# Routed layers of a decoder: more buffers for gathered rows, selected matrices stored token by token, gates and fetches at other places in the order

## The chip, the cores and the metric

The kernel runs on one core of one Trainium2 chip. The metric is the device time of one execution in microseconds (us), and of several executions the median. The core has five engines that run side by side and wait for each other through semaphores: PE (matrix products, with PEld for the load of its stationary operand), DVE (vector), ACT (scalar, activation functions), POOL (GpSimd) and SP, which here only issues DMAs. Transfers between memory and on-chip buffers are DMAs; those that one engine issues leave its queue in order.

## The reference

A decoder of twelve blocks on x of 32 batches x 128 tokens x 128 features, all in fp32. Each block is `x = x + f(layernorm(x))`. The change touches the sixth, a pair of routed layers (and the place where a small filter for the seventh is computed). Eight rows of 128 features make one routed "token" of 32 x 32 numbers, so there are 512 routed tokens:

```python
def kmoe(x_flat, W_router, A, B, scale, bias, d_in1, d_in2, d_out1, d_out2, top_k):
    logits = x_flat @ W_router.T                  # 64 experts
    vals, idx = jax.lax.top_k(logits, top_k)      # the best 2
    probs = jax.nn.softmax(vals, axis=-1)
    xs = x_flat.reshape(-1, d_in1, d_in2)
    Ag = A[idx]
    Bg = B[idx]
    Y = jnp.einsum('nkoi,nij,nkpj->nkop', Ag, xs, Bg)
    out = jnp.einsum('nkop,nk->nop', Y, probs).reshape(-1, d_out1 * d_out2)
    return out * scale + bias
...
    h = kmoe(x_flat, W_up, A_up, B_up, scale_up, bias_up, D1, D2, F1, F2, TOP_K)      # 32x32 -> 64x64
    h = jax.nn.gelu(h, approximate=False)
    y = kmoe(h, W_down, A_down, B_down, scale_down, bias_down, F1, F2, D1, D2, TOP_K) # 64x64 -> 32x32
```

So every token is multiplied from both sides by the matrices of its two experts, weighted by their shares, first upwards (32 x 32 to 64 x 64) and then downwards.

## The kernel before

The kernel runs the twelve blocks one after the other. Stages up to the fifth run in `stream` (L1493), the routed pair in `l1_ffn` (L2616), the seventh in `l2_attn` (L3059). Here tokens are worked in four blocks k = 0 to 3 of eight batches (128 routed tokens each, one to a partition where tokens lie on partitions), and a block in four quarters m = 0 to 3, each of two batches f.

**Routing upwards** is `routing(k)` (L2554), a generator that does a share of its work at each call. It normalizes eight batches (`xn`), transposes them (`xp`), multiplies by the router (`lp`), takes the best two (`top`), and then, on POOL, gathers the rows of the experts' table by eight indirect DMAs (`whole`, two buffers, L2603), each of which SP stores to a table in memory (`tup`, L2604), one row per token. The shares of the two experts are kept as `R`. For blocks 0 and 1 the shares run inside `stream` (L1798 to L1802), on the steps t at which u is 0, 1, 2, 3, 5, 6 and 7; for blocks 2 and 3 `routed(k)` (L2641) runs the whole of it at one place in `l1_ffn`.

**Upwards product** of a block:

- `fetched(k, m)` (L2645) reads a quarter of the block's table back, with four DMAs of 256 KB issued by SP, into two `gt` tiles. Four such tiles exist.
- `gated(k)` (L2655) spreads the shares `R` over partitions with one matmul (`pr`) and copies them to `gate` on DVE. It also takes the block's buffer for `h`, of which there are two.
- `blocks(k, m)` (L2663) transposes the tokens (DVE) and writes them as block diagonals `bd` (ACT).
- `inner(k, m)` (L2674) multiplies them by one of the matrices (PE, `tp`), and DVE multiplies by `gate` on the way out of PSUM (`tb`). `tp`, `pr`, `xp`, `lp` and the filters' products share two PSUM tiles (`bank`).
- `outer(k, m)` (L2687) multiplies by the other matrix (PE, `hp`, 32x64 pieces); DVE adds the bias into `h`, ACT applies Gelu.

`first(k)` (L2804) runs these for the four quarters; `inner` runs one quarter ahead, and a quarter m + 2 is fetched when `outer(k, m)` is issued.

**Routing downwards**: `logits(k)` (L2706) multiplies `h` by the second router (`lp`), `chosen(k)` (L2719) takes the best two as one-hot rows `oh`, `marked(k)` (L2733) transposes them (`op`, 64x64 matmuls on two diagonal quarters of the array).

**Downwards product**, `second(k)` (L2821):

- `picked(k, n)` (L2753), eight times: a matmul of a slice of all experts' matrices (`tab`, read by `tables`, three buffers) with the one-hot rows gives the chosen experts' matrices of every token (`gp`, a PSUM tile of 128 x 1024). ACT and DVE in turn copy it to `gd[0]` (n < 4) or `gd[1]`.
- `narrowed(k, m, w)` (L2763), eight times: 16 matmuls of 64x64 (`td`; each is two records in the profile), stationary `h` of a token, moving that token's matrix from `gd[0]`. ACT copies the result to `tb` (two copies, tile `td`).
- `spread(k, m, w)` (L2777): 32 matmuls (`yp`; 64 records), stationary that token's matrix from `gd[1]`, moving `tb`.
- `returned(k)` (L2790): DVE transposes `yp` back, adds it to x and takes the statistics of the eight batches for the next layer norm.

In `gd` of before the token is the last axis, so one token's matrix has its elements 64 (and 128) numbers apart:

```python
gd = [one.tile([128, 32, 2, 64], F32, name=f"gd{j}") for j in range(2)]   # [.., column, expert, token]
```

**What sets the order.** `Ordered` (L1355) makes every engine's compute instructions run in the order of the program text; DMAs are placed in SP's queue by a scheduler, mostly as they become ready. So the list at the end of `l1_ffn` (L2836 to L2872) is the order of PE, DVE, ACT and POOL.

**The filters** (`filters`, L3015) compute the seventh block's long filter in three shares, called from `l1_ffn`: loads, then a product `fa` and a sine, then a product `hp1` with a decay and a store to `flt`. They have a pool of their own for `pe`, `tw`, `fw1`, `fw2`, `row`, `arg`, `turn`, `dec` and `w`.

Of the kernel before, what the change touches and what calls it, by code (L numbers as in the profile page):

```python
# [13 lines left out]
F32 = mybir.dt.float32  # L14
# [1352 lines left out]
class Fast(General):  # L1367
# [125 lines left out]
    def stream(self, stages, context=False, fresh=False):  # L1493

        tc, plain = self.tc, self.nc
        nc = self.nc = Ordered(plain, tc)
        M = NB * len(stages)
        with ExitStack() as es:
# [274 lines left out]
            for t in range(-9, M + 11):  # L1773
                n = t - 3
                if 0 <= n < M and n % 2 == 1:
                    outputs(n)
                for fn, at in after:
                    n = t - at
                    if n % 4 == 3 and 0 <= n < M:
                        fn(n // 4)  # L1780
                if context and -3 <= t < NB - 3 and t % 4 == 1:
                    context_group((t + 3) // 4)
                for fn, at in ahead:
                    n = t + at
                    if n % 4 == 0 and 0 <= n < M:
                        if fn is normed and n % NB == 0:
                            T[n // NB] = self.prepared(wk, bank, *stages[n // NB])
                        fn(n // 4)
                if 0 <= t - 1 < M:
                    summed(t - 1)  # L1790
                if 0 <= t < M:
                    scores(t)
                for n in (t - 2, t - 1):
                    if 0 <= n < M and (T[n // NB]["kind"] == "keys") == (n == t - 2):
                        values(n)
                if fresh:
                    for k in range(2):
                        u = t - (M - NB + 8 * k + 13)  # L1798
                        if u == 0:
                            T["route", k] = self.routing(k, bank)  # L1800
                        if u in (0, 1, 2, 3, 5, 6, 7):
                            next(T["route", k], None)  # L1802
        self.nc = plain

# [811 lines left out]
    def l1_ffn(self):  # L2616
# [4 lines left out]
        with ExitStack() as es:  # L2621
# [13 lines left out]
                nc.sync.dma_start(out=t, in_=i[key])  # L2635
                return t

            gd = [one.tile([128, 32, 2, 64], F32, name=f"gd{j}") for j in range(2)]
            A, B, C, D = self.A, {}, {}, {}

            def routed(k):  # L2641
# [3 lines left out]
            def fetched(k, m):  # L2645
                s = A[k]
                for f in range(2):
                    j = 2 * m + f
                    s["gt"][j] = gt = wk.tile([128, 4, 2, 128], F32, tag="gt", name="gt", bufs=4)
                    for c in range(2):  # L2650
                        nc.sync.dma_start(out=gt[:, :, c, :],
                                          in_=s["tab"][c, 16 * j:16 * j + 16].rearrange("(g r) (i c) -> (r i) g c", g=4,
                                                                                        c=128))

            def gated(k):  # L2655
                s = A[k]
                p = bank([128, 64], "pr")
                self.mm(p, self.bg("lup"), s["R"].rearrange("p g k -> p (g k)"))
                s["gate"] = wk.tile([128, 64], F32, tag="gate", name="gate")
                nc.vector.tensor_copy(s["gate"], p)  # L2660
                B[k] = wk.tile([128, 64, 64], F32, tag="h", name="h")

            def blocks(k, m):  # L2663

# [88 lines left out]
            def picked(k, n, eng):  # L2753

                t = T.pop(8 * k + n)
                p = banks([128, 8, 128], "gp")
                for c in range(8):
                    self.mm(p[:, c, :], t[:, c, :], D[k][:, 2 * (n // 4):2 * (n // 4) + 2, :].rearrange("p c t -> p (c t)"))
                eng(gd[n // 4][:, 8 * (n % 4):8 * (n % 4) + 8].rearrange("p c k t -> p c (k t)"), p)
                if 8 * k + n + 3 < 32:  # L2760
                    tables(8 * k + n + 3)

            def narrowed(k, m, w):  # L2763
                h = B[k]
                t0 = 16 * m + 8 * w
                tp = banks([128, 2, 512], "td")
                for u in range(8):
                    for f in range(2):
                        q = slice(64 * f, 64 * f + 64)
                        self.mm(tp[q, f, 64 * u:64 * u + 64], h[q, t0 + u, :],  # L2770
                                gd[0][q, :, :, t0 + u].rearrange("p c k -> p k c"))
                D[k, m, w] = tb = wk.tile([128, 16, 32], F32, tag="td", name="td")
                for f in range(2):
                    q = slice(64 * f, 64 * f + 64)
                    nc.scalar.copy(tb[q], tp[q, f].rearrange("p (u c) -> p u c", c=32))

            def spread(k, m, w):  # L2777
                tb = D.pop((k, m, w))
                if m == w == 0:
                    D["y"] = banks([128, 2, 512], "yp")  # L2780
                yp = D["y"]
                for u in range(8):
                    for c in range(2):
                        for f in range(2):
                            q = slice(64 * f, 64 * f + 64)
                            g, r = 2 * w + u // 4, u % 4
                            self.mm(yp[32 * r:32 * r + 32, f, 128 * m + 32 * g:128 * m + 32 * g + 32],
                                    gd[1][q, :, c, 16 * m + 8 * w + u], tb[q, 2 * u + c, :], start=c == 0, stop=c == 1)

            def returned(k):  # L2790
                yp = D.pop("y")
# [10 lines left out]
                    self.stats(self.X[:, 8 * k + j, :], 8 * k + j)  # L2802

            def first(k):  # L2804
                gated(k)
                inner(k, 0)
                for m in range(4):
                    if m < 3:
                        inner(k, m + 1)
                    if m == 1 and k > 0:  # L2810
                        marked(k - 1)
                    if m < 2:
                        blocks(k, m + 2)
                    outer(k, m)
                    if m < 2:
                        fetched(k, m + 2)
                    if k == 0 and m < 2:
                        next(taps)
                A.pop(k)

            def second(k):  # L2821
# [11 lines left out]
                        marked(3)  # L2833
                returned(k)

            fetched(0, 0)  # L2836
            fetched(0, 1)
            bup, tdn, iota = load("bup", [128, 64]), load("c_tdn2", [128, 64]), load("c_iota", [128, 64])
            wdn = load("wdn", [128, 64, 64])
            taps = self.filters(es, bank)  # L2840
            next(taps)
            for n in range(3):
                tables(n)
            blocks(0, 0)
            blocks(0, 1)
            first(0)
            fetched(1, 0)
            fetched(1, 1)
            routed(2)
            blocks(1, 0)  # L2850
            blocks(1, 1)
            logits(0)
            chosen(0)
            first(1)
            fetched(2, 0)
            fetched(2, 1)
            routed(3)
            blocks(2, 0)
            blocks(2, 1)
            logits(1)  # L2860
            second(0)
            first(2)
            fetched(3, 0)
            fetched(3, 1)
            blocks(3, 0)
            blocks(3, 1)
            logits(2)
            second(1)
            first(3)
            logits(3)  # L2870
# [141 lines left out]
                    normed(g + 2)  # L3012


    def filters(self, es, bank):  # L3015

        nc, tc, i = self.nc, self.tc, self.i
        fp = es.enter_context(tc.tile_pool(name="L2af", bufs=1))
        pe = fp.tile([33, 2, 128], F32, name="pe")
        nc.sync.dma_start(out=pe, in_=i["c_pe"])  # L3020
        tw = fp.tile([128, 2, 128], F32, name="tw")
        nc.sync.dma_start(out=tw, in_=i["c_tw"])
        fw1 = fp.tile([33, 64], F32, name="fw1")
        nc.sync.dma_start(out=fw1, in_=i["fw1"])
        fw2 = fp.tile([64, 256], F32, name="fw2")
        nc.sync.dma_start(out=fw2, in_=i["fw2"])
        row = fp.tile([128, 2, 256], F32, name="row")
        nc.gpsimd.memset(row, 0.0)
        yield
        ap = bank([64, 256], "fa")  # L3030
        self.mm(ap, fw1, pe.rearrange("p n t -> p (n t)"))
        arg = fp.tile([64, 256], F32, name="arg")
        nc.vector.tensor_scalar(arg, ap, self.col("L2a_b1")[0:64], 10.0, ALU.add, ALU.mult)

        turn = fp.tile([64, 256], F32, name="turn")
        nc.vector.tensor_scalar(turn, arg, 1.0 / (2.0 * math.pi), None, ALU.mult)
        nc.vector.tensor_scalar(turn, turn, 12582912.0, None, ALU.add)
        nc.vector.tensor_scalar(turn, turn, 12582912.0, None, ALU.subtract)
# [1 line left out]
            nc.vector.scalar_tensor_tensor(arg, turn, -part, arg, ALU.mult, ALU.add)  # L3040
        nc.vector.tensor_scalar(arg, arg, 3.1415925, -3.1415925, ALU.min, ALU.max)
        nc.scalar.activation(arg, arg, AF.Sin)
        dec = fp.tile([128, 2], F32, name="dec")
        for n in range(2):
            nc.scalar.activation(dec[:, n:n + 1], self.col(f"L2a_fd{n}"), AF.Exp)
        nc.vector.tensor_scalar(dec, dec, -1.0, None, ALU.mult)
# [1 line left out]
        for n in range(2):  # L3048
            hp = bank([128, 128], "hp1")
            self.mm(hp, fw2[:, 128 * n:128 * n + 128], arg[:, 128 * n:128 * n + 128])  # L3050
            w = fp.tile([128, 128], F32, name=f"w{n}")
            nc.scalar.activation(w, tw[:, n, :], AF.Exp, scale=dec[:, n:n + 1])
            nc.vector.scalar_tensor_tensor(w, hp, self.col(f"L2a_b2{n}"), w, ALU.add, ALU.mult)
            nc.vector.tensor_scalar(row[:, n, 127 * n:127 * n + 128], w, self.col(f"L2a_fb{n}"), 1.0 / 128.0,
# [182 lines left out]
```

## Time and profile before

| what | value |
|---|---|
| runs | 5709.6, 5717.45, 5721.61 us; median 5717.45 us |
| profiled execution | 5707.47 us, its span 5705.6 us |
| PE busy over the span | 5085.8 us (89%) |
| routed layers in the span | 807 to 1232 us |
| first(0), first(1), first(2), first(3): first `tp` to end of last `hp` | 816.3 to 857, 877.9 to 925.7, 1001.6 to 1038.9, 1094.0 to 1134 us |
| logits(0) to (3) start | 867.3, 935.6, 1041.3, 1135.5 us |
| second(0), second(1): first `gp` to end of last `yp` | 945.1 to 1001.4, 1050.8 to 1093.7 us |
| second(2), second(3) | 1145.0 to 1187.9, 1187.9 to 1230.4 us |

The profile is of one execution; times in it count from the span's start. A row of its timeline gives start and length in us, the engine, the line of the program, the operation with the names of what it writes and reads, its shape and a count, and in brackets how long the engine was idle before it and what ended that. L1350 is a helper through which most instructions pass, and L363 is another, so rows are told apart by their tiles. PE's rows of a group overlap, so the distance from the start of one group to the start of the next says more than the length of one record.

### The profile page before, as it was taken

What the parts mean: (1) busy time and instruction counts of PE and PEld (TensorE: products, weight loads), DVE (VectorE), ACT (ScalarE), POOL (GpSimd) and SP (SyncE); (2) the same over time, 40 slices, a digit from 0 to 9 for tenths busy, and PEclk for the clock granted to TensorE, in tenths of its full rate; (3) what the DMA queues carried; (4) which work ended last, traced back from release to release, by engine and by line L of the source; (5) the groups of instructions that cost most, each with busy time, mean ns of one, the idle gap of its engine ahead of it and who ended that gap; (6) DMA issues with size and microseconds to landing.
All of it is one profiled execution on the core that took longest, in us unless ns stands there. A gap on an engine that the chain in (4) does not pass through costs nothing.

```text
span 5705.6 us, 143617 instructions
## 1 busy us (share of the span) xinstructions
PE 5085.8 (89%) x56814; PEld 3543.7 (62%) x56814; DVE 4246.9 (74%) x11606; ACT 2931.8 (51%) x4110; POOL 3053.6 (54%) x4772
## 2 busy tenths in 40 slices
PE   8976976777877999886899999999999999999998
PEld 4533556664555666664666666666666666676665
DVE  5577642345529999986888888888888888888885
ACT  5756752233525555543455555555555555555554
POOL 0042011011014555555777778778778777777774
PEclk9988987798989999998999999999999999999999
DMA  1000055233002222211334444444444444444442
GB/s 50 2 1 1 2 182 190 83 94 111 9 11 57 51 50 52 51 46 47 65 63 83 83 76 70 76 82 72 72 84 74 72 82 75 72 71 71 74 72 54
DMA packets 1807432, 376.01 MB, mean 66 GB/s; under 512 B 1681459, under 2 KB 1786394, under 8 KB 1805727
## 3 DMA queue, kind: packets, MB, share of 16 engines
q1 hardware_dynamic: 1797376, 330.90, 28.6%
q10 hardware_dynamic: 4766, 19.06, 1.0%
q0 software_dynamic: 4608, 16.78, 0.9%
q8 instruction: 451, 7.39, 0.6%
q14 instruction: 231, 1.88, 0.1%
HBM read 124.02 MB, written 41.16 MB: 29 GB/s over the span
## 4 chain that ended last, share of the span: by engine, by line
PE 37%; DVE 11%; SPq 7%; POOL 5%; DMA 4%; issue 3%; ACT 2%; DVEq 0%; ACTq 0%; POOLq 0%
SPq L2039 7%; PE sc L1350 6%; PE y L1350 6%; PE qk L1350 5%; PE av L1350 5%; PE vp L1350 4%; DMA qkT<-bt 3%; POOL rt L1350 2%; POOL raw L1350 2%; DVE bt L1350 2%; PE gp L1350 2%; PE oTp L1350 2%; PE ap L1350 1%; DVE neg L1350 1%; DVE ss L1350 1%
## 5 line engine op out<-in xcount | busy, mean ns | idle before, releaser
L1350 POOL TENSOR_TENSOR raw<-raw,rt 128x1024 f32<-128x1024 f32 x384 | 899.0, 2362 | 0.0
L1350 POOL TENSOR_TENSOR raw<-raw,ry 128x2048 f32<-128x2048 f32 x224 | 811.3, 3622 | 14.0
L1350 PE MATMUL qk<-wqkv,zs 128*128 128x512 f32 x1536 | 724.3, 594 | 7.5 <-DVE raw L1350 7.5
L1350 ACT ACTIVATE sq<-qk 128x1024 f32<-128x1024 f32 x448 | 458.6, 1024 | 362.9 <-PE qk L1350 152.5
L1350 POOL TENSOR_TENSOR rt<-ry 128x32 f32<-128x32 f32 (+1 forms) x864 | 198.7, 230 | 797.2 <-DVE ry L1350 688.6
L1350 DVE TENSOR_REDUCE ss<-sq 128x16 f32<-128x1024 f32 x448 | 532.9, 1194 | 46.7 <-ACT sq L1350 46.7
L1350 DVE TENSOR_TENSOR rt<-qk,tab 128x1024 f32<-128x1024 f32 x384 | 468.6, 1220 | 61.3 <-ACT sq L1350 43.3
L1350 DVE STREAM_TRANSPOSE bt<-raw 128x1024 f32<-128x1024 f32 x384 | 455.0, 1221 | 69.2 <-POOL raw L1350 45.0
L1350 DVE TENSOR_TENSOR raw<-qk,tab 128x1024 f32<-128x1024 f32 x384 | 466.9, 1216 | 0.0
L1350 ACT ACTIVATE PT<-sc 128x1024 f32<-128x1024 f32 x384 | 373.0, 1027 | 139.4 <-PE sc L1350 139.1
L1350 PEld LDWEIGHTS qk<-wqkv,zs 128*128 128x128 f32 x1536 | 273.9, 191 | 263.4 <-issue 254.7
L1350 ACT ACTIVATE P<-sc 128x1024 f32<-128x1024 f32 x384 | 373.2, 1021 | 117.4 <-PE sc L1350 116.8
L1350 ACT COPY oT<-oTp 128x512 f32<-128x512 f32 x384 | 208.3, 588 | 438.1 <-PE oTp L1350 437.9
L1350 PE MATMUL sc<-qkT 64*128 64x128 f32 x6144 | 406.8, 283 | 7.5 <-DMA qkT<-bt 1.5
L1350 PEld LDWEIGHTS sc<-qkT 64*128 64x128 f32 x6144 | 374.1, 193 | 59.0 <-issue 53.3
L1350 PE MATMUL vp<-wqkv,zs 128*128 128x512 f32 x768 | 404.5, 608 | 1.4 <-DVE raw L1350 1.4
L1350 PE MATMUL av<-va,P 128*64 128x65 f32 x12288 | 401.1, 223 | 0.0
L1350 PE MATMUL y<-wo,oT 128*128 128x128 f32 x3072 | 392.4, 281 | 0.0
L1350 PEld LDWEIGHTS y<-wo,oT 128*128 128x128 f32 x3072 | 364.7, 193 | 42.2 <-issue 24.8
L1350 PEld LDWEIGHTS av<-va,P 128*64 128x64 f32 x12288 | 374.5, 137 | 23.2 <-issue 0.2
L1350 ACT COPY va<-vp 128x1024 f32<-128x1024 f32 (+1 forms) x232 | 218.0, 940 | 214.3 <-PE vp L1350 214.1
L1350 POOL TENSOR_TENSOR X<-X,brep 128x512 f32<-128x512 f32 x24 | 30.5, 1271 | 512.4 <-DVE xn L1350 512.4
(414 smaller groups left out, 10768.5 us busy)
## 6 DMA issues: line engine op xcount, KB each, us to landing
qkT<-bt SPq DMA_DIRECT2D x3072, 64.0 KB
rows<-scr SPq DMA_DIRECT2D x32, 672.0 KB
tup<-whole SPq DMA_DIRECT2D x32, 512.0 KB
gt<-tup SPq DMA_DIRECT2D x64, 256.0 KB
tab<-in_tdo SPq DMA_DIRECT2D x32, 512.0 KB
T<-flt SPq DMA_DIRECT2D x16, 1024.0 KB
wqkv<-in_dqkv ACTq DMA_DIRECT2D x6, 1536.0 KB
scr<-dots SPq DMA_DIRECT2D x128, 66.0 KB
```

The source lines that it names most:

```text
L1350: self.last = call(*a, **k)
L2039: nc.sync.dma_start(out=qkT[r:r + 32, :, j, :], in_=bt[32 * j:32 * j + 32, o])
```

## The change

- `gt` has six buffers in place of four. `fetched(k, 0)` to `fetched(k, 2)` are called ahead of `first(k)`, and `fetched(k, 3)` inside it after `outer(k, 0)`. For blocks 2 and 3 the three calls stand between `logits(k - 1)` and `second(k - 2)`.
- `gd` has the token as its first axis, then expert, then column. The copies out of PSUM still read it from end to end, so that two neighbours in PSUM (one column of two tokens) are written 64 numbers apart; `narrowed` and `spread` read one token's matrix as contiguous numbers.
- `gated(k)` is called ahead of the block: for block 0 before the fetches, for 1 before `logits(0)`, for 2 and 3 after `logits(1)` and after `first(2)`. The buffer for `h` is now taken in `first(k)`.
- `routed(3)` moves from before `blocks(2, 0)` to between `second(0)` and `first(2)`.
- `filters` keeps its tiles as pieces of one `h` buffer (`room`) in place of a pool; its loads follow the first three fetches in the text, where `bup`, `tdn` and `iota` stand between them.
- In `stream` the shares of `routing` run at u = 0 to 6 with no step left out.

```diff
-                        if u in (0, 1, 2, 3, 5, 6, 7):
+                        if 0 <= u < 7:
                             next(T["route", k], None)
...
-            gd = [one.tile([128, 32, 2, 64], F32, name=f"gd{j}") for j in range(2)]
+            gd = [one.tile([128, 64, 2, 32], F32, name=f"gd{j}") for j in range(2)]
...
-                    s["gt"][j] = gt = wk.tile([128, 4, 2, 128], F32, tag="gt", name="gt", bufs=4)
+                    s["gt"][j] = gt = wk.tile([128, 4, 2, 128], F32, tag="gt", name="gt", bufs=6)
...
                 nc.vector.tensor_copy(s["gate"], p)
-                B[k] = wk.tile([128, 64, 64], F32, tag="h", name="h")
...
-                eng(gd[n // 4][:, 8 * (n % 4):8 * (n % 4) + 8].rearrange("p c k t -> p c (k t)"), p)
+                eng(gd[n // 4][:, :, :, 8 * (n % 4):8 * (n % 4) + 8].rearrange("p t k c -> p c k t"), p.rearrange("p c (k t) -> p c k t", k=2))
...
                         self.mm(tp[q, f, 64 * u:64 * u + 64], h[q, t0 + u, :],
-                                gd[0][q, :, :, t0 + u].rearrange("p c k -> p k c"))
+                                gd[0][q, t0 + u])
...
-                                    gd[1][q, :, c, 16 * m + 8 * w + u], tb[q, 2 * u + c, :], start=c == 0, stop=c == 1)
+                                    gd[1][q, 16 * m + 8 * w + u, c, :], tb[q, 2 * u + c, :], start=c == 0, stop=c == 1)
...
             def first(k):
-                gated(k)
+                B[k] = wk.tile([128, 64, 64], F32, tag="h", name="h")
...
                     outer(k, m)
-                    if m < 2:
-                        fetched(k, m + 2)
+                    if m == 0:
+                        fetched(k, 3)
...
+            gated(0)
             fetched(0, 0)
+            bup, tdn, iota = load("bup", [128, 64]), load("c_tdn2", [128, 64]), load("c_iota", [128, 64])
             fetched(0, 1)
-            bup, tdn, iota = load("bup", [128, 64]), load("c_tdn2", [128, 64]), load("c_iota", [128, 64])
+            fetched(0, 2)
+            taps = self.filters(wk.tile([128, 64, 64], F32, tag="h", name="room"), bank)
+            next(taps)
             wdn = load("wdn", [128, 64, 64])
-            taps = self.filters(es, bank)
-            next(taps)
...
             first(0)
-            fetched(1, 0)
-            fetched(1, 1)
+            for m in range(3):
+                fetched(1, m)
             routed(2)
             blocks(1, 0)
             blocks(1, 1)
+            gated(1)
             logits(0)
             chosen(0)
             first(1)
-            fetched(2, 0)
-            fetched(2, 1)
-            routed(3)
             blocks(2, 0)
             blocks(2, 1)
             logits(1)
+            gated(2)
+            for m in range(3):
+                fetched(2, m)
             second(0)
+            routed(3)
             first(2)
-            fetched(3, 0)
-            fetched(3, 1)
+            gated(3)
             blocks(3, 0)
             blocks(3, 1)
             logits(2)
+            for m in range(3):
+                fetched(3, m)
             second(1)
...
-    def filters(self, es, bank):
+    def filters(self, room, bank):
...
+        room = room.rearrange("p t c -> p (t c)")
+        at = [0]
+
+        def piece(n, *shape):
+            size = math.prod(shape)
+            at[0] += size
+            t = room[0:n, at[0] - size:at[0]]
+            return t if len(shape) == 1 else t.rearrange("p (a b) -> p a b", a=shape[0])
+
-        pe = fp.tile([33, 2, 128], F32, name="pe")
+        pe = piece(33, 2, 128)
```

The other tiles of `filters` become pieces in the same way.

More of the change, by code (lines that the diff above doesn't have):

```diff
@@ L3012, in l2_ffn @@
                     normed(g + 2)
-    def filters(self, es, bank):
+    def filters(self, room, bank):
         nc, tc, i = self.nc, self.tc, self.i
-        fp = es.enter_context(tc.tile_pool(name="L2af", bufs=1))
-        pe = fp.tile([33, 2, 128], F32, name="pe")
+        room = room.rearrange("p t c -> p (t c)")
[6 more added lines that the diff above has]
+        pe = piece(33, 2, 128)
         nc.sync.dma_start(out=pe, in_=i["c_pe"])
-        tw = fp.tile([128, 2, 128], F32, name="tw")
+        tw = piece(128, 2, 128)
         nc.sync.dma_start(out=tw, in_=i["c_tw"])
-        fw1 = fp.tile([33, 64], F32, name="fw1")
+        fw1 = piece(33, 64)
         nc.sync.dma_start(out=fw1, in_=i["fw1"])
-        fw2 = fp.tile([64, 256], F32, name="fw2")
+        fw2 = piece(64, 256)
         nc.sync.dma_start(out=fw2, in_=i["fw2"])
-        row = fp.tile([128, 2, 256], F32, name="row")
+        row = piece(128, 2, 256)
         nc.gpsimd.memset(row, 0.0)
@@ L3031, in filters @@
         self.mm(ap, fw1, pe.rearrange("p n t -> p (n t)"))
-        arg = fp.tile([64, 256], F32, name="arg")
+        arg = piece(64, 256)
         nc.vector.tensor_scalar(arg, ap, self.col("L2a_b1")[0:64], 10.0, ALU.add, ALU.mult)
-        turn = fp.tile([64, 256], F32, name="turn")
+        turn = piece(64, 256)
         nc.vector.tensor_scalar(turn, arg, 1.0 / (2.0 * math.pi), None, ALU.mult)
@@ L3042, in filters @@
         nc.scalar.activation(arg, arg, AF.Sin)
-        dec = fp.tile([128, 2], F32, name="dec")
+        dec = piece(128, 2)
         for n in range(2):
@@ L3050, in filters @@
             self.mm(hp, fw2[:, 128 * n:128 * n + 128], arg[:, 128 * n:128 * n + 128])
-            w = fp.tile([128, 128], F32, name=f"w{n}")
+            w = piece(128, 128)
             nc.scalar.activation(w, tw[:, n, :], AF.Exp, scale=dec[:, n:n + 1])
```

## The prediction

> **What bounds the kernel now.** The page's slices place the routed layers (L1 FFN) at 807 to 1232 us of the span; PE is their engine, at a lower clock than around them. The waits of PE in 805:1235 say what it lacks (waiter, releaser, us in total, times, longest):
>
> ```profile
> PE tp L1350 <- DMA gt<-tup: 54.0, 10, 14.4
> PE gp L1350 <- DMA tab<-in_tdo: 15.1, 11, 7.5
> PE tp L1350 <- DVE gate L1350: 11.6, 3, 5.1
> ```
>
> Gathered rows that have not landed cost PE 54.0 us. The stage windows then set second(0) beside second(1), the same work (length, then busy us and count of PE, PEld, DVE, ACT and POOL, granted clock, DMA share, GB/s):
>
> ```profile
> 945.10:1001.40 56.30, 44.83 (x903) 42.16 (x901) 7.33 (x18) 15.53 (x21) 7.98 (x7) 0.88 0.57 198
> 1050.80:1093.70 42.90, 40.85 (x903) 38.49 (x900) 7.33 (x18) 16.66 (x22) 0.00 (x0) 1.00 0.33 101
> ```
>
> Where routed(3) gathers beside it, second(0) takes 13.4 us more; where nothing does, PE is busy 40.85 of 42.90 us. There the matmuls themselves count. The timeline of PE in second(2) (start, us, count at the end):
>
> ```profile
> 1175.07 1.35 PE L1350 MATMUL yp<-td,gd 64*32 64x32 f32 x64
> 1176.34 0.68 PE L1350 MATMUL op<-ident,oh 64*64 64x64 f32 x16
> 1176.86 1.92 PE L1350 MATMUL td<-gd,h 64*64 64x64 f32 x32
> 1178.71 1.33 PE L1350 MATMUL yp<-td,gd 64*32 64x32 f32 x64
> ```
>
> op and td are the same 64x64 f32 product on the same two diagonal quarters of the array. From the start of op's loads (1176.34) to those of td (1176.80) is 0.46 us, 28.8 ns for each of 16; td runs from there to 1178.71, 59.7 ns each of 32. td differs in one thing: its moving operand is read from gd with 256 and 512 bytes between elements.
>
> **Selected matrices token by token.** A block k has 256 td records (8 x 32). If contiguous reading gives them op's rate, that is 256 x (59.7 - 28.8) = 7.9 us; the bound on the other side is 0. yp reads gd as its stationary operand, 512 records a block at 1.26 us per 64 (1208.54 to 1209.80), 19.7 ns. The nearest contiguous small product is hp (32x64), 128 in 1.46 us, 11.4 ns; so yp saves 0 to 8.3 ns, and I take 3.7 ns, 1.9 us, nearer to no gain because the other strided stationary operand (yp of L3144, 32 loads in 1.04 us) is hardly slower than the contiguous u of L2979 (28 in 0.80, 28.6 against 32.5 ns). Two gaps come back: td no longer covers ACT's two copies of td (1.19 us and 0.17 to start), 0.4 us ahead of the first yp and 0.6 ahead of the last, 1.0 us.
>
> The price is the 8 gd copies, which now write every element 256 bytes from the last:
>
> ```profile
> L3156 DVE TENSOR_TENSOR X<-yt,X 128x512 f32<-128x512 f32 x16 | 19.3, 1217 | 28.0 <-PE yt L3153 28.0
> L1350 DVE COPY gd<-gp 128x1024 f32<-128x1024 f32 x16 | 19.5, 1222 | 36.5 <-PE gp L1350 36.5
> L1350 ACT COPY gd<-gp 128x1024 f32<-128x1024 f32 x16 | 16.2, 1012 | 73.2 <-PE gp L1350 73.2
> ```
>
> L3156 writes (and reads) with 512 bytes between elements: 2.38 ns an element against 1.19 for the copy. Bounds: no change, or double, 2.4 us on DVE and 2.0 on ACT; I take double. PE makes a gp in 1.8 us and each engine copies every other one, so 2.4 of 3.6 us is covered by three PSUM tiles; only the copy behind chosen (n = 5) ends late, 17.65 us into the block where td wants its tile at 17.4: 0.35 us a block. Net 7.9 + 1.9 - 1.0 - 0.35 = 8.4 us a block, **33.6 us** in four.
>
> The Trainium skill ("TensorE: Matmul & The Clock Gate", "Wait — 56ns, not 53.3ns?") speaks against the yp part: starts of matmuls never come closer than about 25 ns however short they are. The hp row, 11.4 ns, denies that here; by the rule yp would save nothing and the sum would end 7.6 us higher. Another page ("SBUF — State Buffer", Door 1) has 16-byte lines with a penalty for every access that leaves one, which would slow ACT's copies too; no row here has ACT writing so, and the page gives no size.
>
> **Fetched rows, gate, order.** Times run forward through the stage. In the changed program's SP queue fetches of gt stand thus: (0,0) to (0,2) at once; (0,3), (1,0) to (1,2) all before the stores of routed(2); (1,3) behind five and six of these; (2,0) to (2,2) behind all; then the tabs of second(0); then two stores of routed(3), three DMAs of (2,3), two stores, the fourth of (2,3), and the rest.
>
> First(0): the four filter loads went ahead of gt on SP (809.99 to 812.21); now gt goes first, 2.2 us. The rest of first(0) hangs on the filters' chain DVE-ACT-DVE (arg, Sin, dec, w with table loads between), which I leave, plus 0.5: **2.7 us**. Nothing hides these loads' new place, but fa wants them only at 830; and the h buffer they lie in is read last by the flt store, issued at 848, while block 1 writes it from 886.
>
> First(1): gate's 1.4 us and the 14.4 us wait for (1,2) go. Next late is (1,3), whose DMAs take the queue places that (1,2)'s had (issued 894.79 and 897.17; tp at 901.75 and 905.30 to 907.3). With the start 2.7 earlier inner(1,3) ends at 904.6, and hp of 2 and 3 take 6.4 us (919.3 to 925.7): 911.0 against 925.7, 14.7, of which 2.7 is counted: **12.0 us**.
>
> Routed(3) leaves its place: logits(1) began 9.9 us after first(1) ended (925.7 to 935.59); without it, it waits 2.4 us for the last Gelu (as 1038.9 to 1041.27) and 0.4 for the gate's matmul: **7.1 us**. Second(0) loses its neighbour: 13.4, less 1.0 for the gt loads that now land beside it: **12.4 us**.
>
> Routed(3) at its new place, counted from the end of second(0)'s last yp: returned(0) holds DVE 6.1 us (1001.47 to 1007.6), the root 2.4, then xp, as at 928.44 to 935.6, 7.2: lp ends at 16.1. First(2) runs m = 0 to 2 by 27. But the fourth DMA of (2,3) stands behind the fourth store of gathered rows; gathers start at 17.5 and the fourth store left 18.6 us after the first gather (937.40, 956.06). It is issued at 36.1, lands 4.6 later (897.17 to 901.75), then tp 2.0 and hp 4.9: 47.6, against 37.6 (1001.35 to 1038.9). **Loss 10.0 us**; the gate ahead gains nothing here. The stores behind clear by 57, ahead of second(1)'s first new tab at 59.
>
> First(3): gate is ready, but tb still queues on DVE behind returned(1), to 6.2 us; hp(0) ends at 12.3 (13.4 before), (3,2) is there, (3,3) is issued at 12.4 and lands by 16.2 (1107.23 to 1111.05 then). Ends at 23, lp at 25.6 against 41.75 (1093.73 to 1135.48): **16.0 us**.
>
> Earlier shares of routing(0) and (1) cost and bring nothing: their gathers already waited for rows (8.8 and 9.1 us idle on POOL) and then for their two buffers. X<-X,brep slides behind four gathers, some 17 us on POOL; its reader X<-X,y comes some 17 steps of 3.6 us later.
>
> **Sum.** 33.6 + 2.7 + 12.0 + 7.1 + 12.4 - 10.0 + 16.0 = 73.8 us. The profiled execution took 5707.47 (span 5705.6 and 1.9 around it), so 5633.7; it lies 10.0 below the median of 5717.45. Against the median: **5644 us**. Later stages keep their order and move earlier as a whole.
>
> **Rivals.** *The stride is not what slows td.* For it: td waits for nothing else, but its array tiles alternate otherwise than op's within u. Then the layout gives nothing and costs 1.4: 73.8 - 33.6 - 1.4 = 38.8 gained, 5679. *The gathers hold the fetches.* For it: SP is one queue and (1,3), (2,3) stand behind gathers whose pairs take some 10 us. If both wait one pair longer and second(0) keeps half its loss, 10 + 10 + 6.2 fall away: 47.6 gained, 5670. *Slower: copies to strided addresses become the bound.* Place: picked, DVE with four copies and some 3 us of chosen in 17.4 us. It shows above (17.4 - 3)/4 = 3.6 us a copy, and undoes 73.8 us when a block gets 18.5 us longer, at (17.4 + 18.5 - 3)/4 = 8.2 us, 8 ns an element; at 8.5 us the time is 5722 or more, at 10 us 5746. The only strided row has 2.38. *The queue does not do what it says* is the second rival.
>
> **Numbers.** Forecast 0.64 (own range 5612 to 5664: yp at hp's rate gives 17 - 7.6 = 9 us more, and a gather chain without neighbours some 10 to 20), stride 0.14, gathers 0.12, slower copies 0.06, no change 0.04 (both first rivals, 12.6 us left, with copies near 4 us). Faster by over 0.2% (about 11 us, what a measurement of this kernel can tell from no change) 0.90, within 0.04, slower 0.06. The range takes in the first two rivals: 5612 to 5686.
>
> **What would show it.** Right: td near 29 ns a record and yp below 20; gd copies near 2.4 (DVE) and 2.0 us (ACT); second blocks of 34 to 35 us at clock 1.0; PE's wait for gt down from 54 to some 25 us, most in first(1) and first(2); none for gate. Wrong: td still near 60 ns; gd copies above 3.6 us; PE waiting in picked; first(2) longer than 50 us after second(0).

## The result and the profile after

The changed kernel takes 5675.1 us (median of 5666.02, 5673.17, 5677.04 and 5678.12), beside 5719.19 us for the kernel before: a ratio of 0.9924, 95% interval 0.9908 to 0.994. It is faster by some 44 us; the forecast was 73.8. The profiled execution took 5678.12 us, its span is 5676.3.

Two profiled executions differ outside the routed layers too, by up to 17 us (below), so I compare the stage itself: from PE's first `pr` row to the end of its last `yp`. It lasted 423.2 us before (807.2 to 1230.4) and 373.1 after (811.6 to 1184.7): 50.1 us less. The kernel after, profiled a second time, had 372.7. The places at which the parts below begin and end are rounded to 0.1 us. The last `hp` of first(0), first(1) and first(3) before ends at 856.1, 924.4 and 1133.2 us (the table ahead of the prediction has 857, 925.7 and 1134).

| part of the stage, us | before | after | gained | forecast |
|---|---|---|---|---|
| start to end of first(0) | 48.9 | 41.3 | 7.6 | 2.7 |
| to end of first(1) | 68.3 | 56.7 | 11.6 | 12.0 |
| to second(0) | 20.7 | 12.1 | 8.6 | 7.1 |
| second(0) | 56.3 | 39.7 | 16.6 | 12.4 + 8.4 |
| first(2) | 37.5 | 51.1 | -13.6 | -10.0 |
| logits(2) | 11.9 | 11.8 | 0.1 | 0 |
| second(1) | 43.0 | 43.1 | -0.1 | 8.4 |
| first(3), logits(3) | 51.2 | 39.3 | 11.9 | 16.0 |
| second(2) | 42.9 | 39.2 | 3.7 | 8.4 |
| second(3) | 42.5 | 38.8 | 3.7 | 8.4 |
| sum | 423.2 | 373.1 | 50.1 | 73.8 |

Outside the second blocks 26.2 us came, where 27.8 were forecast. In the four second blocks 23.9 came, where 46.0 were forecast. The waits of PE in the routed layers after (waiter, releaser, us in total, times, longest):

```profile
PE tp L1350 <- DMA gt<-tup: 19.7, 6, 8.7
PE yp L1350 <- issue: 15.7, 13, 2.2
PE xp L1350 <- DVE xn L1350: 12.9, 2, 8.9
...
PE gp L1350 <- DMA tab<-in_tdo: 7.9, 10, 3.0
```

The wait for gathered rows fell from 54.0 to 19.7 us and that for gate is gone, both as forecast. New is the second line: `yp` waits 15.7 us for *issue*, that is, for nothing that the profile shows. The timeline of PE in second(3) after (start, us, then the count and the idle time ahead of the row) says where:

```profile
1166.29 1.15 PE L1350 MATMUL td<-gd,h 64*64 64x64 f32 x32
1167.37 0.75 PE L1350 MATMUL yp<-td,gd 64*32 64x32 f32 x58
1169.40 0.31 PE L1350 MATMUL yp<-td,gd 64*32 64x32 f32 x6 [1.28 <-issue]
1169.64 1.15 PE L1350 MATMUL td<-gd,h 64*64 64x64 f32 x32
1170.72 0.81 PE L1350 MATMUL yp<-td,gd 64*32 64x32 f32 x64
1171.46 1.02 PE L1350 MATMUL td<-gd,h 64*64 64x64 f32 x26
1172.88 0.44 PE L1350 MATMUL td<-gd,h 64*64 64x64 f32 x6 [0.39 <-issue]
1173.25 0.82 PE L1350 MATMUL yp<-td,gd 64*32 64x32 f32 x64
1173.99 1.15 PE L1350 MATMUL td<-gd,h 64*64 64x64 f32 x32
1175.07 0.37 PE L1350 MATMUL yp<-td,gd 64*32 64x32 f32 x26
1176.62 0.54 PE L1350 MATMUL yp<-td,gd 64*32 64x32 f32 x38 [1.19 <-issue]
```

Both products became faster: 32 td in 1.08 us (1166.29 to 1167.37), 33.8 ns each where it was 59.7; 64 yp in 0.74 us (1173.25 to 1173.99), 11.6 ns where it was 19.7. But PE stops in the middle of a group, and in these rows always after the same number of records: 6 + 32 + 64 + 26 = 128 from 1169.40 to the next stop, 6 + 64 + 32 + 26 = 128 from 1172.88 to the one after. So td and yp of a block take 21.6 us (1163.08 to 1184.7) where they took 25.5, though the array needs only 256 x 33.8 + 512 x 11.6 ns = 14.6 us.

The copies to gd are longer, as forecast (from the groups with their shapes kept apart):

```profile
L1350 ACT COPY gd<-gp 128x1024 f32<-128x1024 f32 x16 | 30.8, 1926 | 58.7 <-PE gp L1350 58.7
...
L1350 DVE COPY gd<-gp 128x1024 f32<-128x1024 f32 x16 | 30.3, 1916 | 26.8 <-PE gp L1350 26.7
```

ACT 1012 to 1926 ns, DVE 1222 to 1916. Both still wait for PE ahead of a copy, so they cost next to nothing: the eight gp of second(3) take 17.2 us (1145.92 to 1163.08), and took 17.0.

### The profile page after: what moved, and what is told of

Its sections match the earlier page's. It is cut to its first block, busy times and chain, and to the rows that moved or that the text cites. A ratio compares the mean times of both kernels' runs of the same rounds, so it can differ in the third digit from the quotient of the medians.

```text
span 5676.3 us, 143617 instructions
## 1 busy us (share of the span) xinstructions
PE 5058.5 (89%) x56814; PEld 3507.2 (62%) x56814; DVE 4265.4 (75%) x11606; ACT 2940.2 (52%) x4110; POOL 3060.3 (54%) x4772
## 3 DMA queue, kind: packets, MB, share of 16 engines
q8 instruction: 451, 7.39, 0.6%
## 4 chain that ended last, share of the span: by engine, by line
PE 35%; DVE 11%; SPq 9%; POOL 5%; DMA 4%; issue 4%; ACT 2%; DVEq 0%; ACTq 0%; POOLq 0%
SPq L2039 8%; PE sc L1350 6%; PE y L1350 5%; PE qk L1350 5%; PE av L1350 4%; PE vp L1350 4%; DMA qkT<-bt 3%; POOL rt L1350 2%; DVE bt L1350 2%; POOL raw L1350 2%; PE gp L1350 2%; PE oTp L1350 2%; PE ap L1350 1%; DVE ss L1350 1%; PE tp L1350 1%
## 5 line engine op out<-in xcount | busy, mean ns | idle before, releaser
L1350 DVE STREAM_TRANSPOSE bt<-raw 128x1024 f32<-128x1024 f32 x384 | 455.6, 1222 | 75.5 <-POOL raw L1350 44.3
```

What stands on the lines that cost most here:

```text
L1350: self.last = call(*a, **k)
```

## The experiments

The theory formed from these rows is **supply**: with the stride gone, PE runs dry of instructions. The page lists the transfers that carry them:

```profile
span 5676.3 us, 143617 instructions
...
q8 instruction: 451, 7.39, 0.6%
```

The trace's records of this queue are packets of 16384 bytes, and in the last 21.5 us of the stage five of them are all that q8 moves. PE has 56814 matmul and 56814 load instructions; 7.39 MB over these are 65 bytes each, so a packet holds 256 instructions, that is 128 records with their loads: the distance between the stops. A packet came every 3.4 to 3.8 us there, some 14 ns an instruction, or 21.5 us for the 1536 of a block's td and yp. The rival is the prediction's own theory, in which the **array** sets the time of these records.

### The layout alone

```diff
 # the kernel before, with
-gd = [one.tile([128, 32, 2, 64], F32, name=f"gd{j}") for j in range(2)]
+gd = [one.tile([128, 64, 2, 32], F32, name=f"gd{j}") for j in range(2)]
 # and its one write (picked) and two reads (narrowed, spread) as in the kernel after
```

> The kernel before with one part of the change alone: the selected matrices gd stored token by token (four lines). The prediction's theory (the time of a block's td and yp records is the array's, set by the stride of their operands) puts this part at 8.4 us a block, 33.6 us in all: 5685 us beside 5719, a ratio of 0.994. The theory formed after the result (with the stride gone, the supply of instructions to PE is the bound: about 14 ns for each of the 1536 instructions of a block's td and yp, 21.5 us where the part took 25.5) puts it at about 4 us a block, 12 to 17 us in all: 5702 to 5707 us, 0.997 to 0.998. The rival that the stride is not what slows td puts it at nothing or at 1 to 3 us a block lost to the slower copies: 5719 to 5731 us.

Measured: 5701.95 us beside 5719.76, a ratio of 0.9967 (0.9956 to 0.9978), 17.8 us; the stage 407.4 us, 15.8 less than before. That is just above what supply gives and half of what the prediction did. In the four blocks the td and yp part took 20.9 to 22.1 us, where it had taken 25.6 to 26.1: 17.2 us less in all.

### All but the layout

```diff
 # the kernel after, with
-gd = [one.tile([128, 64, 2, 32], F32, name=f"gd{j}") for j in range(2)]
+gd = [one.tile([128, 32, 2, 64], F32, name=f"gd{j}") for j in range(2)]
 # and its write and reads as in the kernel before
```

> The kernel after with the old layout of gd: six buffers, gate rows ahead, filters in the free buffer and the new order alone. If the parts add, the prediction's theory (layout worth 33.6 us) gives 5675 + 34 = 5709 us, 0.998 of the kernel before; the theory of instruction supply (layout worth 12 to 17 us) gives 5687 to 5692 us, 0.995, and then the fetching and the order carry most of the gain. The rival that the layout is worth nothing gives 5675 us.

Measured: 5690.63 us, 0.9949 (0.9935 to 0.9963), 29.1 us less than before; the stage 387.4 us. With the new layout 14.3 us of stage follow. The parts add: 15.8 + 35.8 = 51.6 in the stage, 50.1 together.

### Every yp twice

```diff
-                for u in range(8):
+                for u in [u for u in range(8) for _ in range(2)]:
                     for c in range(2):          # in spread
```

> The kernel after with each token's yp matmuls issued twice over (the second pair overwrites the first with the same sums): 512 more matmuls, 1024 more instructions a block, and no other change. Theory of the array's time: 512 x 11.6 ns = 5.9 us a block, 24 us in all: 5699 us. Theory of instruction supply, 14 ns an instruction: 1024 x 14 = 14.3 us a block, 57 us in all: 5732 us; the waits of PE on nothing but issue in td and yp grow by 8 us a block, and the part takes 36 us where it took 21.6.

Measured: 5727.1 us, 1.0014 (1.0005 to 1.0024), 52.0 us over the kernel after, and 5 short of what supply says. The td and yp part took 34.7 to 36.5 us a block, and PE's waits for issue in td and yp rose from 18.3 to 46.2 us. Its timeline in second(3), where nothing else is fetched:

```profile
1207.66 0.44 PE L1350 MATMUL td<-gd,h 64*64 64x64 f32 x6 [1.07 <-issue]
1208.03 1.51 PE L1350 MATMUL yp<-td,gd 64*32 64x32 f32 x122
1211.13 0.31 PE L1350 MATMUL yp<-td,gd 64*32 64x32 f32 x6 [1.59 <-issue]
1211.37 1.15 PE L1350 MATMUL td<-gd,h 64*64 64x64 f32 x32
1212.45 1.75 PE L1350 MATMUL yp<-td,gd 64*32 64x32 f32 x90
1214.60 0.91 PE L1350 MATMUL yp<-td,gd 64*32 64x32 f32 x38 [0.41 <-issue]
```

From stop to stop 128 records each (6 + 122; 6 + 32 + 90) and 3.47 us each, 27.1 ns a record, whether the records are mostly yp or part td. (Of the eight distances between stops in this block seven are 3.47 us and one is 3.75; in the kernel after they were 3.5 to 4.0.) The page of this kernel:

```profile
span 5713.7 us, 147713 instructions
...
q8 instruction: 467, 7.65, 0.6%
```

4096 more instructions, 16 more packets: 256 in each. And the DMA view of 1201.6 to 1236.3 us has one burst of 19 GB/s in every fourth slice of 0.87 us (9 is a small packet of another queue):

```profile
GB/s 0 0 0 19 0 0 0 0 19 0 0 0 19 0 0 0 19 0 0 0 19 0 0 0 19 0 0 0 19 0 0 0 19 0 9 0 19 0 0 0
```

By the records, a packet lands in some 1 us and PE goes on 1.3 to 1.4 us after that (landed 1206.3, 1209.7 and 1213.2; PE at 1207.66, 1211.13 and 1214.60); the next leaves 1.1 to 1.2 us later. So of the 3.5 us the bytes take about 1; the rest passes between a packet's landing and the next one's start. Supply is shown: the array's theory gave 24 us more, supply 57, and 52.0 came. (A kernel with fewer instructions in this part was not run.)

### td among gp

```diff
-                D[k, m, w] = tb = wk.tile([128, 16, 32], F32, tag="td", name="td")
+                D[k, m, w] = tb = wk.tile([128, 16, 32], F32, tag="td", name="td", bufs=3)
...
-                narrowed(k, 0, 0)
+                    if n > 4:
+                        narrowed(k, (n - 5) // 2, (n - 5) % 2)
                 for m in range(4):
                     for w in range(2):
-                        if (m, w) != (3, 1):
-                            narrowed(k, m + w, 1 - w)
                         spread(k, m, w)
+                        a = 2 * m + w + 3
+                        if a < 8:
+                            narrowed(k, a // 2, a % 2)
```

> The kernel after with the td products of the first three steps put behind gp number 5, 6 and 7 (three td buffers in place of two): the same instructions, but 192 of the dense ones stand among the sparse gp ones. Theory of instruction supply: 192 x 14 ns = 2.7 us a block at most, 5 to 11 us in all: 5664 to 5670 us; waits of PE on nothing but issue shrink. Theory of the array's time: no gain (the same records on the same array), 5673 to 5678 us. Rival: PSUM tiles of gp and td hold each other, 0 to 8 us slower.

Measured: 5668.28 us beside 5713.09, 0.9922 (0.9908 to 0.9935), the ratio of the kernel after; the stage 372.6 us. My expectation was wrong. It counted three groups of td, but the third stands behind the last gp, where it stood; two are among gp now. PE in second(3):

```profile
1161.57 1.15 PE L1350 MATMUL td<-gd,h 64*64 64x64 f32 x32
1162.65 2.05 PE L1350 MATMUL gp<-om,tab 128*128 128x128 f32 x16
1164.63 1.15 PE L1350 MATMUL td<-gd,h 64*64 64x64 f32 x32
1165.71 2.05 PE L1350 MATMUL gp<-om,tab 128*128 128x128 f32 x16
1167.69 1.15 PE L1350 MATMUL td<-gd,h 64*64 64x64 f32 x32
```

The part behind the last gp fell from 21.6 to 18.9 us (1167.8 to 1186.7): 2.7, of which 64 records at 27.1 ns are 1.7. But the gp part grew from 17.2 to 19.9. PE is already busy there, so the two td cost their array time of 1.08 us each, which the stops had hidden. The rest of the 2.7 stands elsewhere: the first three gp took 1.3 us longer, at a granted clock of 0.80 (1147.9 to 1155.0; 1.00 after), and the waits for `tab` were 0.9 shorter. All four second blocks took 159.9 us, after 160.7. td is bound by the array (33.8 ns against 27.1 of supply), yp by supply (11.6 against 27.1): only yp would gain among gp, and it can't go there, because it needs its block's last gp. (One block's yp among the next block's gp was not tried.)

### Six buffers undone

```diff
-                    s["gt"][j] = gt = wk.tile([128, 4, 2, 128], F32, tag="gt", name="gt", bufs=6)
+                    s["gt"][j] = gt = wk.tile([128, 4, 2, 128], F32, tag="gt", name="gt", bufs=4)
```

> The kernel after with four buffers of gathered rows in place of six, all else as in after. Theory (the third quarter's early fetch is what the fetching part of the change lives on): the waits of up to 14.4 us for it in first(1), and its like in first(2) and first(3), come back: 15 to 30 us slower than after, 0.995 to 0.9975 of before. Rival (the last quarter, which stands behind the stores of the routing in SP's queue, is the bound anyway): 0 to 5 us slower, 0.9925 to 0.9935.

Measured: 5708.23 us beside 5715.89, 0.9986 (0.9977 to 0.9995), and 40.6 us over the kernel after on the same chip (5667.67); the stage 407.3 us, 34.2 longer. The waits of PE:

```profile
PE tp L1350 <- DMA gt<-tup: 65.8, 14, 12.0
```

More than before had (54.0), and more is lost than the 15 to 30 us expected. So everything that is not layout needs the six buffers to gain anything: with four, the new order, gate and filters leave the stage at 407.3 us, what the layout alone gives (407.4). Six buffers in the order of before were not run, so how much they bring without the new order is open.

### Gate back

```diff
             def first(k):
+                if k > 0:
+                    gated(k)
...
-            gated(1)
-            gated(2)
-            gated(3)
```

> The kernel after with the gate rows of blocks 1 to 3 taken at the start of first(k) again, not a block ahead. PE's waits for gate were 11.6 us in the kernel before (three, up to 5.1). The prediction's steps put 1.4 us of that to the gate's account in first(1) and nothing in first(2) and first(3), where tb queues on DVE behind the same returned(k) anyway: 1 to 3 us slower than after, 0.9925 to 0.993 of before. Rival (the whole wait comes back): 10 to 12 us slower, 0.994 to 0.9945.

Measured: 5667.58 us, 0.9918 (0.9904 to 0.9931), the time of the kernel after on that chip; the stage 371.7 us. PE waits 5.9 us for gate again (three times, up to 3.9), and loses nothing by it: the 4.9 us that `tp` waits for `tb` in the kernel after are not among the waits of this one. As the prediction had it, or less.

### Last quarters from ACT's queue

```diff
                     for c in range(2):
-                        nc.sync.dma_start(out=gt[:, :, c, :],
+                        (nc.scalar if m == 3 else nc.sync).dma_start(out=gt[:, :, c, :],
```

> The kernel after, with the last quarter's gathered rows (fetched(k, 3)) issued from ACT's DMA queue in place of SP's. Theory of the queue: in first(1) and first(2) these transfers stand on SP behind stores of the routing that are not ready, and PE waits 8.7 + 1.6 us and 3.3 + 5.0 us for them; issued from ACT, which is past its work for the quarter then, the waits go: 10 to 18 us less, 5657 to 5665 us. Rival (the transfers are late because the DMA engines are busy with the gathers, wherever they are issued): the waits stay, 5671 to 5679 us. Second rival: ACT's queue holds its own later work (bd, the copies of td) until the buffers come free: up to 5 us slower.

Measured: 5672.0 us, 0.9911 (0.9895 to 0.9926); the stage 372.0 us, 1.1 less than after. The mechanism is there and the gain isn't. In first(2) the waits for (2,3) fell from 3.3 + 5.0 us to 0.5, and second(1) began 203.1 us into the stage, not 212.7. Its PE:

```profile
1018.63 5.62 PE L1350 MATMUL gp<-om,tab 128*128 128x128 f32 x48
1037.03 6.13 PE L1350 MATMUL gp<-om,tab 128*128 128x128 f32 x32 [12.77 <-DMA tab<-in_tdo]
```

and SP's queue at that time:

```profile
1023.04 1.59 SPq L2604 DMA_DIRECT2D tup<-whole  x2
1024.72 5.98 SPq L2651 DMA_DIRECT2D gt<-tup  x8
1030.80 18.54 SPq L2750 DMA_DIRECT2D tab<-in_tdo  x8
```

The next `tab` stands in SP's queue behind routed(3)'s last stores and eight fetches, so it left at 1030.80 whenever PE came for it. Second(1) lasted 51.6 us (43.1 after), which gives 8.5 of the 9.6 us back. Earlier in the stage the same happens: first(1) became 5.5 us shorter and first(0) 5.0 longer, where ACT stood idle for 3.1 us while it issued the block's last fetches (836.05 to 841.17) and PE waited 4.1 us for ACT's `room` (1.7 after), as the second rival has it.

### routed(3) in shares

```diff
 # in second(k), behind spread(k, m, w)
+                        next(route, None)     # route = self.routing(3, bank) for k == 0
...
             second(0)
-            routed(3)
```

> The kernel after with routed(3) not run whole behind second(0) but in seven shares, one after each of the first seven spreads of second(0). Theory (routed(3) in one piece behind second(0) makes PE wait: 8.9 us for xn behind returned(0), 3.3 + 5.0 us for gt(2,3) behind its stores, 3.0 us for tab in second(1)): most of these 20 us go, less what seven shares add to PE and DVE inside second(0), 2 to 4 us: 5655 to 5663 us beside 5675. Rival (gathers beside second(0) slow PE as they did in the kernel before, 13 us): the gain is eaten, 5670 to 5680 us.

Measured: 5659.69 us beside 5713.09, 0.9907 (0.9891 to 0.9922); the stage 364.6 us, 8.5 less than after. (The intervals of the ratios of this kernel and the one after overlap; the gain shows in the stage, which two profiles of the kernel after have at 373.1 and 372.7.) Second(0) lasts 43.8 us (39.7 after), first(2) 43.4 (51.1), second(1) 38.5 (43.1). The wait of 8.9 us for `xn` is gone, and that for `tab` nearly; the waits for (2,3) are not:

```profile
991.27 2.05 PE L1350 MATMUL tp<-gt,bd 128*128 128x128 f32 x8 [5.50 <-DMA gt<-tup]
1000.34 2.05 PE L1350 MATMUL tp<-gt,bd 128*128 128x128 f32 x8 [7.02 <-DMA gt<-tup]
```

### The edits together

```diff
+                        (nc.scalar if m == 3 else nc.sync).dma_start(out=gt[:, :, c, :],
...
+                        next(route, None)     # routed(3) in shares; its own call goes
...
+                            narrowed(k, (n - 5) // 2, (n - 5) % 2)     # td among gp: in the first kernel alone
```

> The kernel after with three edits together: the last quarter's fetches from ACT's queue, routed(3) in shares inside second(0), and three td products among gp. Alone, the first moved its 10 us of waits for gt to a wait for tab in second(1) of 12.8 us, behind the stores of routed(3). If the shares bring these stores forward, both gains stay: 8 (queue) + 15 (shares) + 5 to 10 (mixing) = 28 to 33 us, 5642 to 5650 us. Rival (the gathers of routing(3) beside second(0) take back what the shares bring): 5660 to 5668 us.

> The kernel after with two of the three edits, without the td products among gp: last quarters from ACT's queue and routed(3) in shares inside second(0). Mixing alone moved nothing in a block (38.8 us with and without). If that holds here too: as with all three, a ratio of 0.988 to 0.990 to the kernel before, 5650 to 5658 us. If mixing did bring its 5 to 10 us: 0.990 to 0.992.

Measured: with all three 5650.77 us beside 5713.09, 0.9887 (0.9872 to 0.9902), stage 359.8 us; with two 5658.06 beside 5715.89, 0.9892 (0.9877 to 0.9907), stage 363.9 us. The queue brings next to nothing beyond the shares (364.6 to 363.9). With mixing the stage is 4.1 us shorter here and was 0.5 shorter alone, but not where mixing acts: the four second blocks took 170.4 us with it and 163.4 without, while first(1) and first(2) took 77.1 and 88.9. No run shows why those two became shorter, and the intervals of the ratios overlap, so what mixing brings is open. All three together make the fastest kernel of this study; their interval lies below that of the kernel after on the first chip and overlaps that of its second measurement.

### The kernel after again

> The kernel after once more, beside the three others on their chip. If the differences of 5 to 15 us between the profiles outside the routed layers (start at 807 to 815 us, rest of 4475 to 4492 us) are from execution to execution, this profile shows other values than the first, with a stage of 372 to 374 us again, and the ratio stays at 0.991 to 0.994. If the 4 us later start belongs to the changed kernel, it is there again.

Measured: 5667.67 us beside 5715.89, 0.9909 (0.9894 to 0.9924). The stage took 372.7 us, the rest behind it 4485.3. Over all profiles the stage began between 807.2 and 815.5 us (before's own order 807.2 and, with the layout alone, 811.8; after's 811.6 and 815.0, and 808.2 with four buffers), and what follows took 4475 to 4492 us, with the same code. So the 4.4 us that the first profile after began later are not shown to be a cost of the change, and before's profiled execution was one of its quick ones.

## Why the prediction was right in sign and wrong in size

- **Layout, 33.6 us: the step that failed.** Measured 14.3 to 17.8 us. The array did its part: td saves 256 x (59.7 - 33.8) = 6.6 us a block (7.9 forecast; inside a group its records do start at op's rate, two every 58 ns, and the change from group to group adds the rest) and yp 512 x (19.7 - 11.6) = 4.1 (1.9 forecast; the range to 8.3 held it). The copies stayed below what I took, and hidden, and PE waited 1.4 us in all four blocks for the copies of td, not 1.0 in each. But the step subtracted the saving from the block as if nothing lay below. Of 10.7 us saved on the array 3.9 arrive (25.5 to 21.6), since 768 records at 27.1 ns are 20.8 us whatever the array does. The bursts that I read the rates from (16 op, 128 hp) are at most one packet long, so they could not show a rate that binds over hundreds of records. The page of before showed the packets of q8 (451), and the step had no term for them.
- **Second(1), 8.4 us forecast, 0.1 lost.** The layout gave 3.4 of it (46.5 us without it), and 3.5 were lost: routed(3)'s stores and the fetches of block 3 ran beside it, and a `tab` behind them came 3.0 us late. The step had the stores clear ahead of the first new tab, and counted nothing for the fetches.
- **First(2), -10.0 forecast, -13.6 measured.** The chain was the right one (returned(0) on DVE, xn, gathers, stores, the last fetch of (2,3)); PE waited 8.9 us for xn and 8.3 for (2,3).
- **First(1) 12.0, routed(3) leaving its place 7.1, second(0) without its neighbour 12.4:** measured 11.6, 8.6 and, in the kernel without the layout, 13.3 (43.0 us for 56.3). Right. The 7.1 took first(1) to end at 925.7, where DVE's last row for `h` ends; its last `hp` ends at 924.4, and the same step from there gives 8.3.
- **Start 2.7:** 7.6 came. The step counted the order of the first loads and no wait for rows. PE's waits for `gt` in first(0) fell from 14.1 to 1.1 us, and a wait of 6.8 for `bd` stands in place of the first; with four buffers first(0) took 46.5 us and waited 12.4 for `gt`. **First(3) 16.0:** 11.9; PE still waits 4.9 us for tb there. The two errors nearly cancel.
- **Gate:** nothing, as the steps had it from first(2) on; in first(1) not even its 1.4.
- **The rivals.** "The stride is not what slows td" gave 5679, near the result, by a wrong mechanism: the stride did slow td, and a second limit took over. The measured 5675.1 us lies outside the range of the forecast itself (5612 to 5664) and inside the whole range only because that takes in the first two rivals, neither of which is what happened: so far it is luck. "The gathers hold the fetches" gave 5670, and has a part: the 3.6 us of first(2) and the wait in second(1), not the 26 it charged. "Copies become the bound" is refuted at 1.92 us a copy. The second blocks took 38.8 to 43.1 us, not 34 to 35, and their clock is not why:

```profile
921.70:961.40 39.70, 33.27 (x902) 30.67 (x901) 10.20 (x20) 18.46 (x22) 0.00 (x0) 0.91 0.35 108
...
1145.90:1184.70 38.80, 31.38 (x908) 28.99 (x896) 13.29 (x30) 17.02 (x20) 0.00 (x0) 1.00 0.23 71
```

At a granted clock of 1.00 second(3) is 0.9 us faster than second(0) at 0.91, and PE is busy for 31.38 of its 38.80 us. Of the 7.4 us idle there, 5.0 are five stops for issue (1.28, 0.39, 1.19, 1.18, 0.93).

## What to carry to other kernels

A saving per record ends where the next limit begins: for many small matmuls in a row, count the instructions and set them against the rate at which their packets come (here 256 in 3.47 us), before adding up what the array saves. A wait marked as issue that returns after a fixed number of records points to that limit. And a transfer moved out of a queue in which it stood behind others shows what stands there next, so follow the queue up to the next block before booking the gain.

## What the runs showed of the hardware

- PE's instructions arrive in packets of 16384 bytes, 256 instructions. Where PE uses them up faster, it runs at 3.47 us a packet in the kernel with every yp twice, 13.6 ns an instruction or 27.1 ns a record with its load, of which the transfer itself is some 1 us.
- The Trainium skill ("TensorE: Matmul & The Clock Gate", "Wait — 56ns, not 53.3ns?") has starts of matmuls no closer than about 25 ns. Records of yp come 11.6 ns apart in bursts, closer than that, and 27.1 ns apart over a long run, by supply. But neighbouring records of yp and hp go to different pieces of the array (`f` and `r` in `spread` and `outer`), so their mean does not test the figure for one piece, and the prediction's "denies that here" says no more than this either.
- The price of a stride, fp32: a 64x64 product's moving operand with 512 bytes between neighbouring elements 59.7 ns a record, without 33.8; a 64x32 product's stationary operand, also with 512, 19.7 and 11.6; a copy of 128x1024 out of PSUM that writes every element 256 bytes from the last 1.93 us on ACT (1.01 without) and 1.92 on DVE (1.22).
